# Attention values transposed on VectorE in 32 by 32 blocks, loaded block-wise, in a two-layer image kernel

## The chip, the cores and the metric

The kernel runs on one core of a Trainium2 chip. The core has TensorE (PE in the profile; its weight loads are PEld), VectorE (DVE), ScalarE (ACT), GpSimd (POOL) and SyncE (SP). SP does no arithmetic here: it issues most of the DMA transfers, one after another, in program order. The metric is the device time of one launch in microseconds (us); less is better. All data is float32.

## The reference

Two layers over an image x of 48 channels and 256 by 256 pixels, each added to its own normalised input. The change lies in the attention of layer 0. What it computes, cut to what matters:

```python
# _gn: each of 16 groups of 3 channels loses its mean and is divided by its deviation
qkv = einsum('bchw,oc->bohw', _gn(x), w_qkv)      # 144 channels
qkv = dwconv3x3(qkv, w_dw)
q, k, v = split(qkv, 3, axis=1)
# unfold: image (4 pixels of padding around) cut into 4 by 4 patches;
# head h gets 6 channels x 16 pixels = 96 rows, one column per patch
q, k, v = heads(q), heads(k), heads(v)            # 8 heads of [96, patches]
q, k = l2norm(q), l2norm(k)                       # over the 96 rows
attn = softmax(einsum('bhcn,bhcm->bhnm', q, k) * temperature, axis=-1)
out = einsum('bhcn,bhnm->bhcm', v, attn)          # [96, patches] of each head
x = x + einsum('bchw,oc->bohw', fold(out), w_proj)
# layer 1: three products over width, height and channels in 64 by 64 windows
x = x + sum_t einsum('bcphqw,wW,hH,cC->bCpHqW', windows(_gn(x)), Ws[t], Hs[t], Cs[t])
```

There are 64 by 64 = 4096 patches that hold pixels (`NT`). The patches of the padding hold zeros and enter each softmax sum as a constant (`NBORDER` times exp of minus the maximum).

## The kernel before

The kernel has three stages. The first normalises x, makes the 144 channels and, for head 0, the depthwise convolution, and writes the patches to DRAM tensors `qkv[h]`. The second is the attention, head by head, with the convolution of the next head woven in. The third is the projection and layer 1.

`qkv[h]` has the shape [3, 3, 7, 96, 640]: which of q, k, v is the second index; each 96-row matrix is cut by patches into 7 chunks (`CH`) of 576 columns (`CN`; the last has 640, and the last 64 columns are left unused in the others). A row of patches, 64 columns of all seven chunks, is written by one `Depthwise(h, r)` object; r runs over 0 to 9, where r = 9 fills only the last 64 columns of the last chunk.

The attention runs over `for h in range(8)`, `for g in range(16)`. One pass g (about 22 us) takes two blocks of 128 query patches. All keys of a head (8 tiles `kt`, of 512 patches each) stay in SBUF, 14 buffers in all, so that six of the next head's fit beside them. The parts of a pass, with the names used below:

- `scores` (L563): 24 matmuls (L337) of 128 queries with 4096 keys into four `big` tiles of PSUM (3 buffers), each followed by an exponential on ACT (L572) into `e`. A pass has two of these: first `scores(h, 2g+1)`, then already the first block of the next pass, `scores(h, 2g+2)`. The queries of pass g lie in `qt`, two buffers, loaded two passes ahead (L674).
- `normalised` (L581): VectorE sums the exponentials and scales the block's 128 by 96 values by the reciprocal: `vn`. It reads `vT`, the values with patches on partitions.
- `load_value` and `turn` (L546, L552): the values lie in `qkv[h]` with the 96 rows outside and patches inside. `load_value` brings 512 patches as a [96, 512] tile `vt` (2 buffers, one or two transfers according to where a chunk ends). `turn` makes four 96 by 128 transposes on TensorE into a PSUM tile `pst` and copies it with ACT to `vT` [128, 4, 96] (9 buffers).
- `weigh` (L594): for each k of 4, 32 matmuls (L601) of the two blocks' exponentials with `vn` into a `big` tile, then VectorE adds it to the sum `oacc` in SBUF (L612; L610 in the first pass of a head). With three `big` buffers, the fourth tile of a pass can be started only when VectorE has added the first.

Between these stand the convolution of head h+1 (`Depthwise`: load of three `pad` pieces at L205, first tap on ACT, eight taps on VectorE at L228, sum of squares, norm, scaling, then the stores to `qkv[h+1]` by POOL at L295) and, in head 0 only, the `Strip` objects (L162) that make the 108 channels of heads 2 to 7: each loads `xs` (L171), runs matmuls into a `big` tile (L177) and stores `ot` to DRAM (L189).

The order on every engine is the one in which the code stands, since the loop lies inside `tc.manual_schedule()` (only what comes ahead of it, `load_query(0, 0)`, the keys and first values of head 0, may be moved by the scheduler). A transfer waits on SP until its buffer is free and its data is written; everything behind it on SP waits too. On SP a pass issues in this order: values of this pass, keys of the next head, queries of pass g+2 (they wait until `scores(h, 2g+1)` has finished with the buffer), `pad`, and in head 0 the strips' stores and loads.

In head 0, `load_value(0, m)` and `turn(0, m)` stand ahead of the loop for m = 0 and 1, and in passes 1 to 6 for m = 2 to 7. For the other heads they stand in passes 11 to 14 of the head before (`CR + 2 <= g < CR + 6`), two tiles in each pass; keys of the next head are loaded in passes 12 to 14 (two tiles each) and in pass 15. `turn` stands behind both `scores` and both `normalised` of its pass, ahead of the four `weigh`.

The transfers that SP issues take their completion semaphores in turn from a set of eight, so that a transfer also waits for the one eight places before it.

Of the kernel before, what the change touches and what calls it, by code (L numbers as in the profile page):

```python
# [8 lines left out]
F32 = mybir.dt.float32  # L9
# [14 lines left out]
HD = C * KK // NH  # L24
# [4 lines left out]
CH = 7  # L29
CR = 9  # L30
# [15 lines left out]
def conv_preact_kernel(  # L46
# [15 lines left out]
    nc = tc.nc  # L62
# [11 lines left out]
    CN = CR * PX  # L74
    t1 = [dram.tile([(h1 - h0) * HC, TR, W + 2], F32, name=f"t1_{h0}") for h0, h1 in GROUPS]
    qkv = [dram.tile([3, 3, CH, HD, CN + PX], F32, name=f"qkv{h}") for h in range(NH)]
# [5 lines left out]
    ident = const.tile([128, 128], F32, name="ident")  # L82
# [15 lines left out]
    for s in range(2):  # L98
        r = slice(s * C, (s + 1) * C)
        for h in range(NH if s == 0 else H0):  # L100
            o = s * M0 + h * HC if h < H0 else (h - H0) * HC
            nc.gpsimd.dma_start(
                out=(wq[r] if h < H0 else wr[0:C])[:, o : o + HC].rearrange("c (z e) -> c z e", z=3),
                in_=w_qkvT.rearrange("c (z h e) -> h c z e", z=3, h=NH)[h],
# [4 lines left out]
    for z in range(3):  # L109
        for j in range(CH):  # L110
            p = (z * CH + j) * 6
# [50 lines left out]
    class Strip:  # L162
# [5 lines left out]
        def load(self):  # L168
            self.xs = cv.tile([64 + C, 2, W], F32, name="xs", bufs=3)
            for s, rows in enumerate(both_halves(xc, 2 * self.j, 2)):  # L170
                nc.sync.dma_start(out=self.xs[s * 64 : s * 64 + C], in_=rows)  # L171
# [129 lines left out]
    NB = NT // 128  # L301
# [101 lines left out]
    with tc.tile_pool(name="xn", bufs=1) as xnp, tc.tile_pool(name="cst", bufs=1) as cst, tc.tile_pool(  # L403
        name="nps", bufs=2, space=PSUM
# [123 lines left out]
    with tc.tile_pool(name="ahead", bufs=2) as ah, tc.tile_pool(name="ae", bufs=3) as ae, tc.tile_pool(  # L528
# [2 lines left out]
        MB = 8  # L531
        NK = NB // MB
        NLATE = 1
        RP = TP // PX * KS
        NG = NB // G
        keys, queries, values, oaccs = {}, {}, {}, {}
# [8 lines left out]

        def load_value(h, m):  # L546

            vt = ah.tile([HD, 4 * 128], F32, name="vt")
            load(vt, qkv[h][2, 2], m * 512, (m + 1) * 512)
            values[h, m] = vt  # L550

        def turn(h, m):  # L552
            ps = one.tile([128, 4, HD], F32, name="pst", tag="one")
            for i in range(4):
                nc.tensor.transpose(ps[:, i, :], values[h, m][:, i * 128 : (i + 1) * 128], ident[:HD, :HD])  # L555
            vT = ah.tile([128, 4, HD], F32, name="vT", bufs=9)
            nc.scalar.copy(vT, ps)
            values[h, m] = vT

        e0 = ao.tile([128, NH * NB], F32, name="e0")  # L560
# [20 lines left out]
        def normalised(h, nb, e, zs):  # L581

            b = h * NB + nb
            zt = asm.tile([128, 1], F32, name="zt")
            nc.vector.tensor_reduce(zt, zs, AX.X, ALU.add)  # L585
            zu = asm.tile([128, 1], F32, name="zu")
            nc.vector.scalar_tensor_tensor(zu, e0[:, b : b + 1], float(NBORDER), zt, ALU.mult, ALU.add)
            rz = asm.tile([128, 1], F32, name="rz")
            nc.vector.reciprocal(rz, zu)
            vn = asm.tile([128, HD], F32, name="vn")  # L590
            nc.vector.tensor_scalar_mul(vn, values[h, nb // 4][:, nb % 4, :], rz)
            return e, vn

        def weigh(h, g, blocks, k):  # L594
# [32 lines left out]
        load_query(0, 0)  # L627
        for m in range(NM):
            load_key(0, m, (nc.scalar, nc.sync, nc.gpsimd)[m % 3])
        for m in range(2):  # L630
            load_value(0, m)
            turn(0, m)

# [6 lines left out]
        with tc.manual_schedule():  # L642
            load_query(0, 1)
            block = scores(0, 0)
            for h in range(NH):
                more = h + 1 < NH
                rows = {r: Depthwise(h + 1, r) for r in range(CR + 1)} if more else {}
                for g in range(NG):
                    p, d, n = rows.get(g - 2), rows.get(g - 1), rows.get(g)

                    if not more and g == 0:
# [1 line left out]
                        early = ExitStack()  # L653
                        pe = early.enter_context(tc.tile_pool(name="pe", bufs=1, side="right"))
                        xts = [pe.tile([P2, RP, W], F32, name=f"xt{t}") for t in range(NX)]
                    if h == 0 and 0 < g <= 6:
                        load_value(0, g + 1)
                    if more and CR + 2 <= g < CR + 6:
                        for m in range(2):
                            load_value(h + 1, (g - CR - 2) * 2 + m)  # L660
                    if more and CR + 3 <= g < CR + 6:
                        for m in range(2):
                            load_key(h + 1, (g - CR - 3) * 2 + m)
# [28 lines left out]
                    if g == 0 and rows:  # L692
                        rows[0].load()

                    if h == 0 and 0 < g <= 6:
                        turn(0, g + 1)
                    if more and CR + 2 <= g < CR + 6:
                        for m in range(2):
                            turn(h + 1, (g - CR - 2) * 2 + m)
                    if g == 0 and h > 0:  # L700
                        for m in range(6, 8):
                            store(h - 1, m)
# [293 lines left out]
```

## Time and profile before

| | us |
|---|---|
| median of 3 runs (3668.67 to 3677.88) | 3673.2 |
| span of the profiled execution | 3669.5 |
| PE busy, of the span | 3466.2 |
| PEld busy | 2907.3 |
| VectorE busy | 2139.8 |
| ScalarE busy | 1873.5 |
| POOL busy | 542.7 |
| mean granted TensorE clock | 0.976 of full |

The span runs from the first to the last instruction of the profiled execution; no further time is listed for that execution. In the table of 40 slices the PE row shows 9 tenths or more from slice 4 to slice 34 (about 290 to 3210 us): this is the attention. The first three slices and the last five belong to the other stages. Busy shares overlap, since engines work side by side. An engine that is not busy may still set the time of what waits for it.

### The profile page before, as it was taken

The numbers are of one execution on the slowest core, as the hardware profiler recorded it, in microseconds if no ns is written. First come the engines' busy times: TensorE is split into PE (matmuls) and PEld (weight loads), VectorE is DVE, ScalarE is ACT, GpSimd is POOL, SyncE is SP. The second block draws the span as 40 slices with busy tenths as digits, with TensorE's granted clock in tenths as the row PEclk, the third lists the DMA queues.
The fourth block names the chain that finished last, engine by engine and source line by source line (L and its number), as shares of the span: only waits on it lengthen the run. The fifth ranks groups of instructions, "written<-read, shape, count | busy, mean of one in ns | idle before, by whom it ended". The sixth has DMA issues, their size and how long they took to land.

```text
span 3669.5 us, 100344 instructions
## 1 busy us (share of the span) xinstructions
PE 3466.2 (94%) x44252; PEld 2907.3 (79%) x44252; DVE 2139.8 (58%) x3518; ACT 1873.5 (51%) x2747; POOL 542.7 (15%) x630
## 2 busy tenths in 40 slices
PE   2869999999999999999999999999999999965998
PEld 1337788889988888889899988888899888833776
DVE  5464674179628952895389439934993222267654
ACT  0235676566646654665466556655664444400332
POOL 2030211012211211121112112211221100010011
PEclk9989999999999999999999999999999999976999
DMA  7455665533322332333233323332333220089674
GB/s 161 154 131 147 180 171 168 158 97 92 94 72 82 98 90 80 83 93 87 78 82 92 94 76 87 86 93 71 94 84 87 65 53 19 15 213 240 116 136 93
DMA packets 275427, 386.49 MB, mean 105 GB/s; under 512 B 77330, under 2 KB 211842, under 8 KB 270952
## 3 DMA queue, kind: packets, MB, share of 16 engines
q1 hardware_dynamic: 235942, 264.95, 27.3%
q0 software_dynamic: 35552, 106.40, 12.6%
q10 hardware_dynamic: 3490, 8.64, 1.1%
q8 instruction: 350, 5.73, 0.7%
q14 instruction: 93, 0.76, 0.1%
HBM read 234.76 MB, written 144.90 MB: 103 GB/s over the span
## 4 chain that ended last, share of the span: by engine, by line
PE 84%; DVE 3%; issue 2%; DMA 2%; ACT 1%; SPq 0%; POOL 0%; ACTq 0%; POOLq 0%; DVEq 0%
PE big L337 37%; PE big L601 36%; PE pb L896 4%; PE pa L874 2%; PE pc L913 2%; DVE acc L228 1%; PE big L177 1%; PE pt L618 1%; PE pn L247 1%; DMA pot<-os__70 1%; PE pst L555 1%; DMA x1s<-pxt 0%; DMA kt<-qkv 0%; DMA t<-ot 0%; DVE ss L243 0%
## 5 line engine op out<-in xcount | busy, mean ns | idle before, releaser
L572 ACT ACTIVATE e<-big,nmx 128x1024 f32<-128x1024 f32 x1024 | 1143.9, 1117 | 878.4 <-PE big L337 617.5
L337 PE MATMUL big<-kt,qt 128*128 128x512 f32 x6144 | 1437.5, 393 | 30.2 <-DMA kt<-qkv 29.3
L601 PEld LDWEIGHTS big<-vn,e 128*64 128x64 f32 x32768 | 1358.6, 137 | 57.8 <-ACT e L572 30.6
L601 PE MATMUL big<-vn,e 128*64 128x96 f32 x32768 | 1388.9, 247 | 6.5 <-DVE oacc L612 3.0
L337 PEld LDWEIGHTS big<-kt,qt 128*128 128x128 f32 x6144 | 1146.3, 188 | 277.3 <-issue 29.2
L612 DVE TENSOR_TENSOR oacc<-big,oacc 128x768 f32<-128x768 f32 x480 | 453.5, 954 | 713.4 <-PE big L601 713.4
L228 DVE SCALAR_TENSOR_TENSOR acc<-pad,dwt,acc 126x1024 f32<-126x1024 f32 x592 | 765.6, 1293 | 39.5 <-ACT acc L209 23.7
L295 POOL DMA_DIRECT2D qkv<-o x72 | 52.7, 732 | 1242.2 <-ACT o L279 1242.2
L585 DVE TENSOR_REDUCE zt<-zs 128x1 f32<-128x4 f32 x256 | 38.5, 150 | 335.7 <-ACT e L572 335.7
L289 POOL TENSOR_TENSOR ol<-o,oh 126x1024 fp32r<-126x1024 f32 x78 | 184.6, 2367 | 311.6 <-DVE ss L243 238.9
L572 ACT ACTIVATION_READ_ACCUMULATOR e<-big,nmx 128x1 f32 x1024 | 196.4, 192 | 0.0
L903 ACT COPY lyt<-pb 128x512 f32<-128x512 f32 x144 | 84.3, 586 | 201.6 <-PE pb L896 201.6
L881 DVE TENSOR_TENSOR lzt<-pa,cbias 128x864 f32<-128x864 f32 (+1 forms) x88 | 137.0, 1628 | 85.3 <-PE pa L874 85.3
L279 ACT COPY o<-acc 126x1024 f32<-126x1024 f32 x74 | 158.6, 2143 | 0.0
L896 PEld LDWEIGHTS pb<-wsb,lzt 128*64 128x64 f32 x2304 | 125.9, 138 | 29.4 <-issue 19.7
L896 PE MATMUL pb<-wsb,lzt 128*64 128x128 f32 x2304 | 141.9, 279 | 2.8 <-issue 1.6
L623 POOL DMA_DIRECT2D os__70<-oo x128 | 64.9, 513 | 534.4 <-ACT oo L621 533.8
L790 PE MATMUL pps<-pot,wp 96*96 96x512 f32 x128 | 78.0, 777 | 55.2 <-DMA pot<-os__70 44.3
L239 ACT ACTIVATE sq<-acc 126x1024 f32<-126x1024 f32 x74 | 78.2, 1057 | 101.6 <-DVE acc L228 101.6
L180 ACT ACTIVATE ot<-big,bias 108x1024 f32<-108x1024 f32 x64 | 68.2, 1110 | 111.1 <-PE big L177 62.8
L209 ACT ACTIVATE acc<-pad,dwt 126x1024 f32<-126x1024 f32 x74 | 84.1, 1137 | 79.9 <-DMA pad<-t 79.9
L243 DVE TENSOR_REDUCE ss<-sq 126x64 f32<-126x1024 f32 x80 | 97.5, 1219 | 24.6 <-ACT sq L239 24.6
(127 smaller groups left out, 1904.8 us busy)
## 6 DMA issues: line engine op xcount, KB each, us to landing
pad<-t SPq DMA_DIRECT2D x238, 254.0 KB
t<-ot SPq DMA_DIRECT2D x128, 217.7 KB
qkv<-ol POOLq DMA_DIRECT2D x78, 336.0 KB, 6.4
qkv<-oh POOLq DMA_DIRECT2D x70, 336.0 KB, 5.6
qt<-qkv SPq DMA_DIRECT2D x176, 96.0 KB
xs<-in_x_dram SPq DMA_DIRECT2D x128, 96.0 KB
os__70<-oo POOLq DMA_DIRECT2D x128, 96.0 KB, 2.1
pot<-os__70 SPq DMA_DIRECT2D x16, 768.0 KB
```

The source lines that it names most:

```text
L209: nc.scalar.mul(self.acc, self.pad[:, 0:KS, 0:W], dwt[:, self.h, 0:1])
L228: nc.vector.scalar_tensor_tensor(self.acc, self.pad[:, dy : dy + KS, dx : dx + W], dwt[:, self.h, tap : tap + 1], self.acc, ALU.mult, ALU.add,
L243: nc.vector.tensor_reduce(self.ss, self.sq.rearrange("p a (x b) -> p x a b", b=KS), AX.XY, ALU.add)
L279: nc.scalar.copy(self.o.rearrange("p (a b) x -> p a b x", a=KS), self.acc.rearrange("p a (x b) -> p a b x", b=KS))
L289: eng.tensor_sub(self.ol, self.o, self.oh.bitcast(F32))
L337: nc.tensor.matmul(ps[:, i, :], lhsT=qt[:, r, q0 : q0 + 128], rhs=kts[2 * j + i][:, r // 2, :], start=(r == 0), stop=(r == 2),)
L572: nc.scalar.activation(e[:, j * 1024 : (j + 1) * 1024], ps.rearrange("p a b -> p (a b)"), AF.Exp, bias=nmx[:, b : b + 1], accum_out=zs[:, ...
L601: nc.tensor.matmul(ps[p : p + 64, j // 4, j % 4 * HD : (j % 4 + 1) * HD], lhsT=e[:, mb * 128 + p : mb * 128 + p + 64], rhs=vn, start=(i == 0),
L612: nc.vector.tensor_add(oaccs[h, k], ps[:, :, : 4 * HD], oaccs[h, k])
L881: nc.vector.tensor_tensor(zv[:, :, y0 : y0 + n, :], pa[:, :, : n * T3 * C].rearrange("p s (y k) -> p s y k", y=n), cbias.rearrange("p (u v ...
L896: nc.tensor.matmul(pb[s * WS : (s + 1) * WS, i, :], lhsT=zts[u][:, t * C + c + i, :], rhs=wsb[:, t, :], start=True, stop=True,)
L903: nc.scalar.copy(yt[:, t, :], pb.rearrange("p i x -> p (i x)"))
```

## The change

Values are loaded eight blocks of 128 patches at a time (`VB = 8`, 1024 patches), so that a head needs four loads instead of eight. The new tile `vt` is [128, 8, 3, 32] in one buffer: partition 32p + c holds, for block i and row group b, row 32b + c of the 32 patches that will stand on partitions 32p to 32p + 31 of that block. One transfer carries 32 rows by up to 8 blocks by 32 patches, and it is cut where a chunk of `qkv` ends. `turn` is then one VectorE instruction on [128, 768], which transposes each 32 by 32 square where it stands: it gives `vT` [128, 8, 96] (5 buffers). The four TensorE transposes and the ACT copy of each old `turn` are gone, and with them the PSUM tile `pst`.

The loads of head 0 now stand ahead of the loop for m = 0 and in passes 1 to 3 for m = 1 to 3; those of the next head in passes 11 to 14, one in each. `turn` keeps its place in the pass. The numbers of transfers by load are 24, 36, 36 and 24, so 120 in a head where there were 14.

```diff
+        VB = 8
...
         def load_value(h, m):
 
-            vt = ah.tile([HD, 4 * 128], F32, name="vt")
-            load(vt, qkv[h][2, 2], m * 512, (m + 1) * 512)
+            vt = ah.tile([128, VB, 3, 32], F32, name="vt", bufs=1)
+            for p in range(4):
+                at = [m * VB * 128 + i * 128 + p * 32 for i in range(VB)]
+                chunk = [min(n // CN, CH - 1) for n in at]
+                for j in sorted(set(chunk)):
+                    i0, i1 = chunk.index(j), VB - chunk[::-1].index(j)
+                    n0 = at[i0] - j * CN
+                    for b in range(3):
+                        src = qkv[h][2, 2, j, b * 32 : (b + 1) * 32, n0 : n0 + 32]
+                        src = bass.AP(src.tensor, src.offset, [src.ap[0], [128, i1 - i0], [1, 32]])
+                        nc.sync.dma_start(out=vt[p * 32 : (p + 1) * 32, i0:i1, b, :], in_=src)
             values[h, m] = vt
 
         def turn(h, m):
-            ps = one.tile([128, 4, HD], F32, name="pst", tag="one")
-            for i in range(4):
-                nc.tensor.transpose(ps[:, i, :], values[h, m][:, i * 128 : (i + 1) * 128], ident[:HD, :HD])
-            vT = ah.tile([128, 4, HD], F32, name="vT", bufs=9)
-            nc.scalar.copy(vT, ps)
+
+            vT = ah.tile([128, VB, HD], F32, name="vT", bufs=NB // VB + 1)
+            nc.vector.transpose(vT.rearrange("p i c -> p (i c)"), values[h, m].rearrange("p i b n -> p (i b n)"))
             values[h, m] = vT
...
-            nc.vector.tensor_scalar_mul(vn, values[h, nb // 4][:, nb % 4, :], rz)
+            nc.vector.tensor_scalar_mul(vn, values[h, nb // VB][:, nb % VB, :], rz)
...
-        for m in range(2):
-            load_value(0, m)
-            turn(0, m)
+        load_value(0, 0)
+        turn(0, 0)
...
-                    if h == 0 and 0 < g <= 6:
-                        load_value(0, g + 1)
-                    if more and CR + 2 <= g < CR + 6:
-                        for m in range(2):
-                            load_value(h + 1, (g - CR - 2) * 2 + m)
+                    if h == 0 and 0 < g < NB // VB:
+                        load_value(0, g)
+                    if more and CR + 2 <= g < CR + 2 + NB // VB:
+                        load_value(h + 1, g - CR - 2)
...
-                    if h == 0 and 0 < g <= 6:
-                        turn(0, g + 1)
-                    if more and CR + 2 <= g < CR + 6:
-                        for m in range(2):
-                            turn(h + 1, (g - CR - 2) * 2 + m)
+                    if h == 0 and 0 < g < NB // VB:
+                        turn(0, g)
+                    if more and CR + 2 <= g < CR + 2 + NB // VB:
+                        turn(h + 1, g - CR - 2)
```

## The prediction

> **What bounds the kernel now.** I read the chain of waits first, then two stretches of it, then SP's own timeline for the same stretch, then the rows of the transfers.
>
> ```profile
> PE 84%; DVE 3%; issue 2%; DMA 2%; ACT 1%; SPq 0%; POOL 0%; ACTq 0%; POOLq 0%; DVEq 0%
> ```
>
> TensorE carries the chain in the attention, with almost no idle time: whatever is taken from PE there is gained, whatever makes PE wait is lost. The merged chain of head 1 shows a pass with two turns and, beside it, one without:
>
> ```profile
> 991.03 11.11 PE big L337 x48
> 1002.15 0.66 PE pst L555 x8
> 1002.81 10.71 PE big L601 x256
> 1013.52 11.11 PE big L337 x48
> ...
> 1128.36 10.96 PE big L337 x48
> ...
> 1150.39 10.96 PE big L337 x48
> ```
>
> The pass with turns lasts 1013.52 - 991.03 = 22.49 us, the one without 22.03. PE never waits for `vt` here: the timeline of SP tells why.
>
> ```profile
> 956.67 8.96 SPq L311 DMA_DIRECT2D vt<-qkv  x3
> 974.25 6.01 SPq L311 DMA_DIRECT2D qt<-qkv  x12
> 980.35 1.93 SPq L311 DMA_DIRECT2D vt<-qkv  x4
> 982.39 11.35 SPq L311 DMA_DIRECT2D kt<-qkv  x12
> 996.74 4.01 SPq L311 DMA_DIRECT2D qt<-qkv  x6
> 1002.51 1.71 SPq L311 DMA_DIRECT2D vt<-qkv  x4
> 1004.27 10.57 SPq L311 DMA_DIRECT2D kt<-qkv  x16
> ```
>
> Values take SP 1.7 to 1.9 us a pass, keys 10 to 11, queries 3 to 6. SP is free 5 to 6 us of 22, and only because the values are cheap. (The 8.96 us of the first row are a wait: its second transfer needs the convolution's store that POOL issues at 961.2, and goes at 964.8.)
>
> **What the change removes.** 256 transposes on PE. In passes 11 to 14 of seven heads: 28 x 0.46 = 12.9 us. In head 0, eight turns of 0.3 to 0.6 us each (0.49 us busy in the timeline): about 2.6. Together -15.5 us. The 64 ACT copies (470 ns each) gave nothing to wait for: ACT is 51% busy and its exponentials wait for PE.
>
> **What it adds on VectorE.** 32 transposes of [128, 768]. No row has one; the nearest is L612's add on the same size (954 ns), the dearest POOL's subtraction of 1024 elements (2367 ns). I take 0.95 us, 30 us in all; in passes 11 to 14 VectorE is busy 5.2 us of 22.5, so this by itself hides; at 2.4 us it would add 1.4 to each of the two late turns of a head below, 20 in all at most, which the range holds. The wait it brings is what matters: the turn waits for all 24 or 36 transfers, and behind it on VectorE stands the add L612 that frees the `big` buffer of the fourth `weigh`.
>
> **What it adds on SP.** 960 transfers for 112, at 128 bytes a run. The engines don't mind: the packet records put a 256-byte packet at 18 ns, and 3072 packets over 16 engines are then at most 3.5 us a load. SP's issue decides. Its rows:
>
> ```profile
> L311 SPq DMA_DIRECT2D vt<-qkv x112: 303/418/730, 288.0 to 2815.9; - x112
> L824 ACTq DMA_DIRECT2D csn<-in_Cs_dram x2: 343/402/462, 3209.4 to 3209.8; - x2
> L857 SPq DMA_DIRECT2D lrt<-x1s x16: 574/866/6269, 3371.1 to 3616.8; - x16
> ```
>
> (min/median/max in ns.) The new form has three dimensions on both sides. From below: 0.30 us (a plain transfer that finds the queue empty). Plain ones in a run go at 0.42 and start 0.47 apart. From above: `lrt`, three dimensions of 64 rows, 0.87 + 0.05 between two. Nearest is `csn`, 48 rows by 3 by 48: the second, with one in front of it, took 0.462, so 0.50 apart. I take **0.50 us a transfer**: 12 us for a load of 24, 18 us for one of 36. Completion records of the old `vt` come 2.3 us after issue in the median; I take 2.2 after the last issue has ended.
>
> The Trainium skill speaks against the change: "DMA: Bandwidth & Descriptors", Rules for kernel authors, says that transfers under 64 KB pay mostly overhead, and its fit is 2.0 us a transfer. By it, unoverlapped, 848 more transfers would be some 1700 us, an estimate from that page. The 16 keys in 10.57 us above show that such overhead overlaps, so only the issue enters my sum.
>
> **A head, step by step**, in us from the start of pass 11 (968.7), a pass being 22.0 without turns: 5.5 for each `scores`, then four `weigh` of 2.64. VectorE reaches the turn at 7.8 of a pass; PE wants the first add by 18.9. Keys go at 0.65 (10.57/16), queries at 0.51.
> - Load 0: from -3.8 (964.8, the store) to 8.2; landed 10.4; turned 11.3. No loss. Queries to 14.3.
> - Load 1: to 32.3, landed 34.5, turned 35.5; PE wants the add by 40.9. No loss. 12 keys to 40.1, queries to 43.2.
> - Load 2: to 61.2, landed 63.4, turned 64.3, added 65.3; wanted at 62.9: PE waits 2.4. 16 keys to 71.6, queries to 74.6, landed 76.8; the second `scores` of pass 14 wants them at 73.9: 3.0 (rounded).
> - Load 3: to 86.6, landed 88.8, added 90.8, wanted 90.3: 0.5. 16 keys to 97.0, the next head's first queries landed at 102.3, wanted at 99.3: 3.0. Key tile 6: 0.4.
>
> SP had 5 to 6 us free a pass and is given 10 to 17 more: the backlog surfaces as late turns and late queries. About 9.5 us a head, seven heads: +66.
>
> **Head 0** has no slack, since the strips hold SP:
>
> ```profile
> 324.04 2.00 SPq L311 DMA_DIRECT2D vt<-qkv  x2
> 329.49 6.56 DVE L228 SCALAR_TENSOR_TENSOR acc<-pad,dwt,acc 126x1024 f32<-126x1024 f32 x5
> 336.06 0.96 DVE L612 TENSOR_TENSOR oacc<-big,oacc 128x768 f32<-128x768 f32 x1
> 338.58 1.97 PE L177 MATMUL big<-xs,wr 48*108 48x512 f32 x8
> ```
>
> In pass 1 the load starts at 324.0, ends at 342.0, is landed at 344.2 and turned at 345.2, and L612 ends at 346.1. The second strip's run wanted that buffer at 339.5: 6.6 late, and some 2 more for L243 and the second add behind it. Twice 8.6 (passes 1, 2), and 2.6 for the 24 of pass 3: +20. At the start, 24 transfers at 288 for three (12 for 1.5 us) put the queries of `load_query(0, 1)` 10.5 us back; they had landed 3.7 ahead of their `scores`: at 296.6 (issued by 294.4, completion records 2.0 to 2.2 later) against 300.3 (41 matmuls in 9.57 us from 295.69, the first 20 of them another block's): +7.
>
> **The clock.** In the projection a PE gap of 4.17 us is followed by half clock:
>
> ```profile
> 3257.80:3262.00 4.20, 0.05 (x1) 0.00 (x0) 4.20 (x6) 0.00 (x0) 0.00 (x0) 0.94 1.10 176
> 3262.00:3268.30 6.30, 6.28 (x8) 2.27 (x9) 6.27 (x4) 0.00 (x0) 0.00 (x0) 0.50 0.90 235
> ```
>
> (bounds, length, PE, PEld, DVE, ACT, POOL busy, granted clock, DMA share, GB/s.) So a stall of over 4 us costs 3 us more: three of them in head 0, +9. Those of 3 us in the other heads: nothing taken; at most 14 x 3 = 42, which the range holds. "TensorE: Matmul & The Clock Gate", What's actually happening, puts the drop at about 3.4 us of idleness and the return after about 3.4 us of work; by that rule the three would cost some 5 instead of 9, an estimate from that page, and the shorter ones nothing.
>
> **Sum**: -15.5 + 7 + 20 + 66 + 9 = +86.5 on a span of 3669.5, so 3756. The median of the runs lies 3.7 above the span, so **3760**.
>
> **Rivals.**
> - *The issue is cheap: the turn leaves PE and nothing waits* (the other side). Needs 0.30 us a transfer all through: then load 1 of pass 1 is added at 338.9, ahead of 339.5, about 3 us of stalls stay in head 0 and 2 at the start, and no backlog forms in the others. -15.5 + 5 gives 3663, with none of these stalls 3658. For it: 303 ns exists. Against: only in transfers that find SP idle. Above 0.30 it is gone. Chance 0.10.
> - *Only head 0 pays.* At 0.47 a transfer and 0.56 a key (0.42 and 0.595 alternating, plus gaps) the same ladder leaves 1.6 us a head: -15.5 + 6 + 17 + 11 + 9 gives 3701; at 0.42 about 3680. For it: 0.47 is the plain form's spacing, and part of the keys' 0.65 is waiting behind POOL's stores. Chance 0.22.
> - *The third dimension is dear*, as in `lrt`: at 0.92 the ladder gives 60 a head (422), 60 in head 0, 17 at the start and some 60 of half clock: 4217; at 0.67 30 a head: 3940. For it: 0.87 follows 0.58 regularly. Against: eight times the runs of a new transfer. Chance 0.18.
> - That the change doesn't do what it says is excluded: the built program has no `pst` and 32 transposes on VectorE.
>
> **How the numbers follow.** The forecast (0.47 to 0.58 us a transfer, 3700 to 3860) has 0.50. Changes within 0.3% (11 us) can't be told from none. Faster than 3662 needs the first rival nearly whole: 0.09. 3662 to 3684: the low end of the second and rest of the first, 0.09. Slower 0.82. The range, 3676 to 3930, leaves out 0.1 below and 0.1 above.
>
> **What would show it.** After: a `vt` spacing on SP near 0.5 in runs of 24 and 36; no `pst`; VectorE idle ahead of L565's transpose, released by DMA `vt`, longest in passes 1 and 2; PE waiting for L612's add (now L620) and for DMA `qt` in passes 13 to 15, none in 1 to 10 of heads 1 and later, which should last 22.0 as before. Head 7 loads no values for a next head and should not change. I am wrong if SP's spacing is 0.3 or 0.9, if a stall moves the strips' loads too, or if the DMA engines, not the issue, delay the landing.

## The result, and the profile after

The changed kernel takes **3920.9 us** (median of 4 runs, 3913.2 to 3926.7) against 3674.1 of the kernel before: a ratio of **1.067** (95% interval 1.065 to 1.069), 6.7% slower. Slower was forecast, and the range held the time, but the forecast of 3760 had +86 where +247 was measured. The profiled execution has a span of 3917.7 us, 248.2 more than before.

The chain that ended last (the page's part 4), first by engine, then by line:

```profile
PE 61%; SPq 16%; DMA 5%; issue 5%; DVE 5%; ACT 1%; POOL 0%; ACTq 0%; DVEq 0%; POOLq 0%
PE big L609 26%; PE big L337 25%; SPq L559 11%; SPq L311 4%; PE pb L901 4%; DVE acc L228 2%; PE pa L879 2%; PE pc L918 2%; PE big L177 1%; DMA t<-ot 1%; DMA qt<-qkv 1%; PE pt L626 1%; DMA x1s<-pxt 1%; DMA pad<-t 1%; DVE oacc L620 1%
```

PE had 84% of this chain; now SP's issuing has 16%, and 11 of them are L559, the new value transfers. Where PE stands idle (busy us, mean ns of one, idle us ahead of it and its main releaser; the same groups of the page, and the new turn):

```profile
L609 PE MATMUL big<-vn,e 128*64 128x96 f32 x32768 | 1425.8, 250 | 115.2 <-DVE oacc L620 113.3
L337 PE MATMUL big<-kt,qt 128*128 128x512 f32 x6144 | 1466.9, 398 | 54.8 <-DMA qt<-qkv 44.4
L565 DVE STREAM_TRANSPOSE vT<-vt 128x768 f32<-128x768 f32 x32 | 31.3, 979 | 375.8 <-DMA vt<-qkv 333.1
L177 PE MATMUL big<-xs,wr 48*108 48x512 f32 x256 | 78.7, 692 | 51.3 <-DMA xs<-in_x_dram 44.4
```

The idle time ahead of these three PE groups was 6.5, 30.2 and 1.4 us before: +183 now. They also run longer for the same count of matmuls: 1388.9, 1437.5 and 64.8 us before, +80 now. These 263 us, less some 19 for the transposes that left PE, make 244 of the 248. The turn itself is cheap, 0.979 us; but VectorE stands 376 us ahead of it. How this looks in head 1, SP first (start, length, transfers, count):

```profile
1073.37 15.50 SPq L559 DMA_DIRECT2D vt<-qkv  x24
1088.97 7.27 SPq L311 DMA_DIRECT2D qt<-qkv  x12
1096.34 22.63 SPq L559 DMA_DIRECT2D vt<-qkv  x36
1119.09 7.22 SPq L311 DMA_DIRECT2D kt<-qkv  x12
1126.40 3.10 SPq L311 DMA_DIRECT2D qt<-qkv  x6
1129.61 20.27 SPq L559 DMA_DIRECT2D vt<-qkv  x36
```

From 1073 to 1199 SP has no gap over 0.35 us left. The four loads of the head take 15.50, 22.63, 20.27 and 15.84 us for 24, 36, 36 and 24 transfers: 0.62 us each (0.61 over all 32 loads). VectorE in the same stretch (the bracket is the idle time before the row and who ended it):

```profile
1120.52 0.98 DVE L565 STREAM_TRANSPOSE vT<-vt 128x768 f32<-128x768 f32 x1 [14.03 <-DMA vt<-qkv]
1121.42 2.65 DVE L620 TENSOR_TENSOR oacc<-big,oacc 128x768 f32<-128x768 f32 x3
```

And PE:

```profile
1109.73 8.14 PE L609 MATMUL big<-vn,e 128*64 128x96 f32 x192
1122.40 5.39 PE L609 MATMUL big<-vn,e 128*64 128x96 f32 x64 [4.52 <-DVE oacc L620]
1127.72 11.46 PE L337 MATMUL big<-kt,qt 128*128 128x512 f32 x48
```

The load ends at 1118.97 on SP, the turn starts at 1120.52, three adds that had queued up behind it run at once, and PE, out of `big` buffers since 1117.9, goes on. Its next 64 matmuls take 5.39 us, twice the usual. The windows say why (bounds, length, PE, PEld, DVE, ACT, POOL busy, granted clock, DMA share, GB/s):

```profile
1117.90:1122.40 4.50, 0.00 (x0) 0.00 (x1) 1.88 (x3) 0.00 (x0) 0.00 (x0) 0.90 0.46 126
1122.40:1125.00 2.60, 2.60 (x32) 2.60 (x34) 1.67 (x2) 0.00 (x0) 0.00 (x0) 0.50 0.45 118
1127.00:1128.00 1.00, 1.00 (x11) 0.78 (x10) 0.16 (x1) 0.00 (x0) 0.00 (x0) 0.50 0.67 181
1129.00:1130.00 1.00, 1.00 (x6) 0.80 (x5) 0.48 (x3) 0.31 (x1) 0.00 (x0) 1.00 0.45 139
```

The clock stays at 0.50 for some 6 us after the stall. So a late turn makes PE wait and then run at half speed for a while.

Where the 248 us lie, by the starts of the score matmuls of each pass (worked out from the traces, after minus before, us; the 1.4 us that are missing in the sum lie behind the attention):

```
                   loop    head 0        head 0         heads 1-6   head 7
                   start   passes 0-10   passes 11-15   together
measured            +3.2      +52.6         +52.6         +140.0     -1.6
of it, by pass:  head 0: 0 +8.0, 1 +9.6, 2 +23.2, 3 +7.0, 4 +2.9, 5 +2.0
                 head 0: 11 +8.2, 12 +13.7, 13 +16.5, 14 +12.0, 15 +2.2
                 head 1: 1 to 10 0.0, 11 -0.7, 12 +6.6, 13 +8.1, 14 +3.3, 15 +5.1
```

### The profile page after: what moved, and what is told of

It reads as the page before. It is cut to its first block, busy times and chain, and to the rows that moved or that the text cites. A ratio compares the mean times of both kernels' runs of the same rounds, so it can differ in the third digit from the quotient of the medians.

```text
span 3917.7 us, 100771 instructions
## 1 busy us (share of the span) xinstructions
PE 3525.0 (90%) x43996; PEld 2938.1 (75%) x43996; DVE 2163.6 (55%) x3550; ACT 1850.2 (47%) x2683; POOL 542.7 (14%) x630
## 3 DMA queue, kind: packets, MB, share of 16 engines
q1 hardware_dynamic: 337062, 265.01, 27.0%
q0 software_dynamic: 35552, 106.40, 11.9%
## 4 chain that ended last, share of the span: by engine, by line
PE 61%; SPq 16%; DMA 5%; issue 5%; DVE 5%; ACT 1%; POOL 0%; ACTq 0%; DVEq 0%; POOLq 0%
PE big L609 26%; PE big L337 25%; SPq L559 11%; SPq L311 4%; PE pb L901 4%; DVE acc L228 2%; PE pa L879 2%; PE pc L918 2%; PE big L177 1%; DMA t<-ot 1%; DMA qt<-qkv 1%; PE pt L626 1%; DMA x1s<-pxt 1%; DMA pad<-t 1%; DVE oacc L620 1%
## 5 line engine op out<-in xcount | busy, mean ns | idle before, releaser
L609 PE MATMUL big<-vn,e 128*64 128x96 f32 x32768 | 1425.8, 250 | 115.2 <-DVE oacc L620 113.3
L609 PEld LDWEIGHTS big<-vn,e 128*64 128x64 f32 x32768 | 1391.8, 139 | 178.0 <-DVE oacc L620 128.4
L337 PE MATMUL big<-kt,qt 128*128 128x512 f32 x6144 | 1466.9, 398 | 54.8 <-DMA qt<-qkv 44.4
L337 PEld LDWEIGHTS big<-kt,qt 128*128 128x128 f32 x6144 | 1164.2, 191 | 318.5 <-issue 51.1
L620 DVE TENSOR_TENSOR oacc<-big,oacc 128x768 f32<-128x768 f32 x480 | 448.5, 950 | 488.0 <-PE big L609 488.0
L565 DVE STREAM_TRANSPOSE vT<-vt 128x768 f32<-128x768 f32 x32 | 31.3, 979 | 375.8 <-DMA vt<-qkv 333.1
L180 ACT ACTIVATE ot<-big,bias 108x1024 f32<-108x1024 f32 x64 | 69.3, 1111 | 202.3 <-DMA t<-ot 102.9
L177 PE MATMUL big<-xs,wr 48*108 48x512 f32 x256 | 78.7, 692 | 51.3 <-DMA xs<-in_x_dram 44.4
```

The lines of the kernel that those rows point to most:

```text
L177: nc.tensor.matmul(ps[:M1, s, :], lhsT=wr[r], rhs=self.xs[r].rearrange("p a b -> p (a b)"), start=True, stop=True)
L337: nc.tensor.matmul(ps[:, i, :], lhsT=qt[:, r, q0 : q0 + 128], rhs=kts[2 * j + i][:, r // 2, :], start=(r == 0), stop=(r == 2),)
L609: nc.tensor.matmul(ps[p : p + 64, j // 4, j % 4 * HD : (j % 4 + 1) * HD], lhsT=e[:, mb * 128 + p : mb * 128 + p + 64], rhs=vn, start=(i == 0),
L620: nc.vector.tensor_add(oaccs[h, k], ps[:, :, : 4 * HD], oaccs[h, k])
```

## The experiments

Theory 1 is that SP's issue of 960 transfers is what is paid. Its rivals: the turn's place on VectorE (2), the bytes or packets on the DMA engines (3). In the diffs `-` is the changed kernel, if nothing else is said. The differences given for each run are against the kernel before, by the columns above; two numbers for head 0 are its passes 0 to 10 and 11 to 15.

**Few large transfers, same turn.** All 32 turns stay; the tile is filled by 4 to 6 transfers.

```diff
-            for p in range(4):
...
-                        nc.sync.dma_start(out=vt[p * 32 : (p + 1) * 32, i0:i1, b, :], in_=src)
+            to = vt.rearrange("p i b n -> p (i b n)")
+            n0 = min(m * VB * 128, NT - 768)
+            load(to[0:HD], qkv[h][2, 2], n0, n0 + 768)
+            load(to[HD:128], qkv[h][2, 2][:, 0:32], n0, n0 + 768)
```

> The turn on VectorE stays as in the changed kernel (32 of 128x768, waiting for a whole load), but a load's 393 KB come in 4 to 6 large plain transfers on SP instead of 24 or 36 small ones; the values stand in another arrangement, so the output is not the reference's. Theory 1 (SP's issue of 960 transfers makes the loss): SP is as free as before the change, so no PE wait for the adds behind the turn in passes 11 to 15 and next to none in head 0; 3655 to 3668 us, that is before less the 15.5 us of transposes and plus a few us in head 0. Theory 2 (the turn's place in VectorE's queue, or its one vt buffer, makes the loss, whatever fills the tile): the time stays at 3890 to 3920. Theory 3 (the bytes on the DMA engines): the bytes are the same, so 3850 to 3920.

Measured: 3652.0 us (one run; before 3672.6), 3 below what was expected; span 3649.9. Start -0.6, head 0 -2.0 and -1.7, heads 1 to 6 -15.9 together. Its groups of PE:

```profile
L337 PE MATMUL big<-kt,qt 128*128 128x512 f32 x6144 | 1437.0, 393 | 31.2 <-DMA kt<-qkv 29.2
L603 PE MATMUL big<-vn,e 128*64 128x96 f32 x32768 | 1387.6, 247 | 8.3 <-DVE oacc L614 4.8 <-DVE vn L593 1.9 <-ACT ot L180 1.6
```

Idle and busy times are within 2 us of those of the kernel before. With the same turns at the same places, and the same bytes, nothing is lost and 19.6 us of span are gained: theory 2 falls, and theory 3 as far as it speaks of bytes. A pass with turns went from 22.49 to 21.8 us.

**As many transfers, turned on TensorE.** Against the kernel before:

```diff
-            load(vt, qkv[h][2, 2], m * 512, (m + 1) * 512)
+            for p in range(4):
+                for b in range(3):
+                    n0 = m * 512 + p * 128
+                    load(vt[b * 32 : (b + 1) * 32, p * 128 : (p + 1) * 128],
+                         qkv[h][2, 2][:, b * 32 : (b + 1) * 32], n0, n0 + 128)
```

> The kernel before, transposes on TensorE kept, with nothing changed but that each of its value loads is cut into 12 or more plain pieces of 32 rows by up to 128 columns: as many transfers on SP as the changed kernel has. Theory 1 (SP's count): the loss comes without any work on VectorE: at 0.5 to 0.6 us a piece 3780 to 3920 us, with PE waiting for DMA vt and DMA qt. Theory 2 (the turn on VectorE): 3670 to 3690, within 0.5% of before.

Measured: 3779.5 us (one run), +107, at the lower end of what was expected; the cut makes 840 transfers. Head 0 +40.0 and +41.8, heads 1 to 6 +26.5. VectorE turns nothing here, so a loss needs no turn on it. Most of it lies in head 0, where the strips' transfers also go through SP. In heads 1 to 6 it is far smaller than the +140.0 of the changed kernel: 120 fewer transfers, their plain form, two buffers for `vt` and the turn's place on PE differ together, and no run separates them.

**As many transfers, but plain.** The source is one run of columns instead of blocks 128 apart:

```diff
-                        src = qkv[h][2, 2, j, b * 32 : (b + 1) * 32, n0 : n0 + 32]
-                        src = bass.AP(src.tensor, src.offset, [src.ap[0], [128, i1 - i0], [1, 32]])
...
+                        src = qkv[h][2, 2, j, b * 32 : (b + 1) * 32, n0 : n0 + (i1 - i0) * 32]
...
```

> The same 960 transfers of the same size on SP, but each source a plain 2-D block (32 rows by one run of 32 to 160 floats), no third dimension; the values stand in another arrangement, so the output is not the reference's. If the count and SP's fixed time per transfer make the loss (theory 1a), a transfer goes at 0.5 to 0.6 us all the same and the time is 3780 to 3900. If the 128-byte runs or the third dimension make the transfer dear (theory 1b), it goes at 0.43 to 0.47 and the time is 3680 to 3740. If the landing of 128-byte packets on the DMA engines is what is waited for (theory 3), SP's spacing stays at 0.62 and yet the time falls to about 3700.

Measured: 3827.3 us (one run). A load of 24 or 36 takes 0.54 or 0.56 us a transfer where the changed kernel's take 0.64 and 0.59. Head 0 +45.2 and +43.4, heads 1 to 6 +64.3. So as many plain transfers at the same places make about 155 of the 247 us; the third dimension, with its 128-byte runs, makes the other third through some 0.05 us a transfer. The issue row of the changed kernel (min/median/max ns):

```profile
L559 SPq DMA_DIRECT2D vt<-qkv x960: 302/430/2988, 291.0 to 3085.1; - x192
```

and of `plain_vt`:

```profile
L560 SPq DMA_DIRECT2D vt<-qkv x960: 302/419/2372, 288.9 to 2991.6; - x192
```

The medians hardly differ, and both are below the forecast's 0.50. The means don't follow them: in the changed kernel 71 of the 960 records are longer than 0.9 us, 1.42 in the mean; they add 0.07 to the mean of 0.548, to which the gap between two records adds 0.04. In `plain_vt` it is 74, and they add as much. Such long records weren't new: in the kernel before, 52 of the 384 key records on SP are longer than 0.9 us (median 0.458, mean 0.622), though none of the 112 value records is. The changed kernel's own excess sits in the 240 transfers of five blocks, 0.60 in the median, where those of one to four blocks have 0.42 to 0.43.

**The same transfers on POOL's queue.**

```diff
-                        nc.sync.dma_start(out=vt[p * 32 : (p + 1) * 32, i0:i1, b, :], in_=src)
+                        nc.gpsimd.dma_start(out=vt[p * 32 : (p + 1) * 32, i0:i1, b, :], in_=src)
```

> The changed kernel with its 960 value transfers issued by POOL's queue instead of SP's; nothing else moves. POOL's plain transfers in the trace take 0.51 us (the output rows of a head) to 1.05 us (the strided stores of queries and keys), and POOL is idle in passes 11 to 15. Theory 1 (SP's queue): SP is freed, the strips' loads, keys and queries run as before. At 0.5 us on POOL a load of 36 takes 18 us, it lands in its own pass, and the time is 3658 to 3690; at 1.05 a load of 36 takes 38 us, longer than a pass, and the loss comes back at 3850 or above through late turns alone, with no late queries. Theory 2 or 3 (the turn's place, or 128-byte packets on the DMA engines): 3900 at either price.

Measured: 3722.0 us, ratio 1.013 (1.010 to 1.016). Head 0 +3.3 and +8.7, heads 1 to 6 +36.3. Four fifths of the loss are gone with SP freed. What is left is neither of the two cases expected:

```profile
L559 POOL DMA_DIRECT2D vt<-qkv x960 | 525.7, 562 | 137.4 <-DVE vT L565 76.6
```

At 0.56 us a record, a load of 36 takes 21.1 us in the mean, as on SP (21.2). It fits in a pass, but the turn that waits for it stands 8 us into the pass. The Trainium skill, "DMA: Bandwidth & Descriptors", Issuing engine by pattern, calls the Sync and Scalar path generally the faster one. For a single transfer the rows agree (median 430 ns against 551); for a load of 36 they show no difference (0.59 us a transfer on both).

**Spread over the passes, then the same with a later turn.** The first moves three of a head's four loads and turns out of the crowded passes 11 to 14 and leaves one in pass 12; the second leaves its loads alone and moves only the turns, by one pass.

```diff
+                    if g in (1, 5, 9):
+                        load_value(h, g // 4 + 1)
+                    if more and g == CR + 3:
+                        load_value(h + 1, 0)
...
+                    if g in (1, 5, 9):
+                        turn(h, g // 4 + 1)
+                    if more and g == CR + 3:
+                        turn(h + 1, 0)
```

> The changed kernel's 960 transfers, all on SP and in the same form, moved in time: in every head value tiles 1, 2 and 3 are loaded and turned in passes 1, 5 and 9 of their own head (four passes ahead of their use), tile 0 in pass 12 of the head before. Theory 1 (SP's backlog in passes 11 to 15): heads 1 to 6 lose their 25 us of stalls each, since passes 1 to 10 have over 10 us of SP free; with 36 transfers at 0.62 in one pass the turn may still be 2 to 6 us late there. Head 0 keeps stalls of some 8 us at the start and in passes 1, 5, 9 and 12: 3665 to 3720. Theory 2 (the turn's place on VectorE): the same 32 waits elsewhere, 3850 or above.

The second, against the first:

```diff
-                    if g in (1, 5, 9):
+                    if g in (2, 6, 10):
                         turn(h, g // 4 + 1)
-                    if more and g == CR + 3:
+                    if more and g == CR + 4:
                         turn(h + 1, 0)
```

> The spread version with each turn one pass behind its load (loads in passes 1, 5, 9 and 12, turns in 2, 6, 10 and 13): the same 960 transfers, the same bursts of 24 and 36 on SP at the same places; only the deadline is later. If a burst of 36 at 0.6 us (22 us, landed 2 later) against a turn 8 us into the same pass made the 12 to 17 us that heads 1 to 6 of the spread version still lose, they now gain 2.7 each as with few transfers, and head 0 loses only what its bursts take from the strips' loads on SP (some 20 to 50): 3665 to 3710. If the bursts delay something else on SP (queries, keys, the convolution's rows), heads 1 to 6 stay slow and the time is over 3750.

Measured: `spread_vt` 3817.6 us (one run), well above what was expected: head 0 +53.4 and +11.4, heads 1 to 6 +75.7. `spread_late` 3744.7 (one run), also above what was expected, by 35: head 0 +54.0 and +11.7, heads 1 to 6 +9.3. Pass 1 of head 1 shows the difference. First SP's timeline of `spread_vt`,

```profile
812.45 24.21 SPq L559 DMA_DIRECT2D vt<-qkv  x36
```

then PE:

```profile
814.19 11.19 PE L337 MATMUL big<-kt,qt 128*128 128x512 f32 x48
825.31 8.14 PE L609 MATMUL big<-vn,e 128*64 128x96 f32 x192
839.82 5.39 PE L609 MATMUL big<-vn,e 128*64 128x96 f32 x64 [6.36 <-DVE oacc L620]
```

The same of `spread_late`, SP:

```profile
812.25 23.83 SPq L559 DMA_DIRECT2D vt<-qkv  x34
```

(the window shows 34 of its 36) and PE:

```profile
812.25 11.19 PE L337 MATMUL big<-kt,qt 128*128 128x512 f32 x48
823.38 10.78 PE L609 MATMUL big<-vn,e 128*64 128x96 f32 x256
```

The same burst, found by an idle SP at the start of the pass, stops PE for 6.36 us where a turn in the same pass waits for it, and not at all where the turn comes a pass later. So no backlog is needed: 36 transfers are longer than the time up to the add. Most of the burst's cost in heads 1 to 6 is its **deadline**. Head 0 is different: its loss didn't move with the turns. There the burst holds up the strips, as SP's timeline of `spread_late` shows in pass 5 of head 0:

```profile
451.14 27.59 SPq L559 DMA_DIRECT2D vt<-qkv  x36
481.93 1.98 SPq L189 DMA_DIRECT2D t<-ot  x4
483.96 2.45 SPq L171 DMA_DIRECT2D xs<-in_x_dram  x4
```

For 30 us no strip is stored or loaded, and pass 5 lasts 19.0 us longer than before.

**Head 0 as before.** `mixed_vt` takes the spread version and lets head 0 load in large transfers and turn on TensorE:

```diff
+            if h == 0:
+                to = vt.rearrange("p i b n -> p (i b n)")[:HD, :512]
+                load(to, qkv[h][2, 2], m * 512, (m + 1) * 512)
...
+            if h == 0:
+                ps = one.tile([128, 4, HD], F32, name="pst", tag="one")
+                for i in range(4):
+                    nc.tensor.transpose(ps[:, i, :], values[h, "vt"][:, i * 128 : (i + 1) * 128], ident[:HD, :HD])
...
```

> Head 0 loads and turns as before the change (large loads, transposes on TensorE); heads 1 to 7 load in small transfers and turn on VectorE, with the tiles in passes 12 (for the next head) and 1, 5 and 9. Theory 1: the strips' passes get back what they had, except pass 12 of head 0, which has 24 small transfers (some 8 us), and the seven heads keep the gain of the transposes less late turns at the 36 transfers: 3658 to 3690. Theory 2: no better than 3800.

Measured: 3775.7 us, ratio 1.027 (1.024 to 1.030): not as expected, since heads 1 to 6 keep the late turns of `spread_vt` (+80.2). Head 0 is as forecast by theory 1: +4.9 in passes 0 to 10 where `spread_vt` had +53.4, and +11.8 in 11 to 15, all of it in pass 12 with its 24 transfers for head 1.

**Fewer transfers by another order of the queries.** A block takes every second patch of its 256, so that one transfer brings 32 rows of all three row groups by 64 patches.

```diff
-                    lhsT=qt[:, r, q0 : q0 + 128],
+                    lhsT=qt[:, r, q0 // 128 : 256 : 2],
...
+                    src = qkv[h][2, 2, j].rearrange("(b c) n -> c b n", b=3)[:, :, n - j * CN : n - j * CN + 64]
+                    dst = to[p * 32 : (p + 1) * 32, u * 192 : (u + 1) * 192].rearrange("p (b n) -> p b n", b=3)
+                    nc.sync.dma_start(out=dst, in_=src)
```

> Loads and turns in the same passes as in the changed kernel and on SP, but 16 transfers for a load instead of 24 or 36 (512 in all): a block of 128 queries takes every second patch of its 256, so that a partition quarter's run is 64 patches and one transfer takes all three row groups. Theory 1: at 0.55 to 0.6 us a load takes 9 to 10 us; the ladder of the prediction, with 16 in place of 24, 36, 36, 24, gives stalls of 0 to 5 us a head, and head 0 some 10 to 40 in all: 3665 to 3725. Theory 3 (what counts is the number of DMA packets, or the turn): over 3800; the packets are halved with runs of 256 bytes, so at least half of the loss, 3790.

`perm4_vt` does the same pass by pass: `load_value(h, g + 2)` behind `load_query(h, g + 2)`, and `turn(h, g + 1)` in every pass.

> The same arrangement, and each pass loads and turns only its own 256 patches, two passes ahead, behind the queries in SP's order: 4 transfers and a turn of 128x192 a pass, 512 and 128 in all. Theory 1: SP is given 2.4 us in each pass, in passes 11 to 14 about what the old values took (1.7 to 1.9), so no backlog forms anywhere, no turn waits, and the transposes' time is gained whole: 3652 to 3668, faster than before by 0.2 to 0.5%. Theory 2 (a turn on VectorE in front of the adds costs by itself): 128 turns, slower than before. If the weight loads of every second column are slow on TensorE, the scores take longer than 5.5 us and the time is far above 3700.

Measured: `perm_vt` 3726.4 us (one run), just above what was expected; `perm4_vt` 3706.1, ratio 1.008 (1.005 to 1.012), not faster as expected but slower. In `perm_vt` PE doesn't wait over 0.8 us anywhere in heads 1 to 6, and a load of 16 takes 8 to 15 us (10.8 in the mean); head 0 still pays +17.7 and +19.3. Both pay in every pass for something else, the weight loads of every second column. The groups of L337 in `perm4_vt`:

```profile
L337 PE MATMUL big<-kt,qt 128*128 128x512 f32 x6144 | 1477.2, 398 | 32.9 <-DMA qt<-qkv 21.9
L337 PEld LDWEIGHTS big<-kt,qt 128*128 128x128 f32 x6144 | 1182.4, 194 | 284.6 <-issue 31.2
```

194 ns a load instead of 188, and 0.3 us in each of the 128 passes (22.03 to 22.33), 38 us in all. 3706 less these 38 is 3668, about the kernel before; a version without them wasn't run.

**More transfers than the changed kernel, evenly.** Blocks are consecutive again; every pass loads its own 256 patches in 8 transfers, two passes ahead.

```diff
-            vt = ah.tile([128, VB, 3, 32], F32, name="vt", bufs=1)
+            vt = ah.tile([128, 2, 3, 32], F32, name="vt", bufs=3)
             for p in range(4):
...
+                for i in range(2):
+                    n = g * 256 + i * 128 + p * 32
+                    j = min(n // CN, CH - 1)
+                    src = qkv[h][2, 2, j].rearrange("(b c) n -> c b n", b=3)[:, :, n - j * CN : n - j * CN + 32]
+                    nc.sync.dma_start(out=vt[p * 32 : (p + 1) * 32, i], in_=src)
...
                         load_query(h, g + 2)
+                        load_value(h, g + 2)
```

> More transfers than the changed kernel has, 1024, all on SP, blocks of 128 queries as they were, but 8 in every pass, two passes ahead of use, behind the queries, and a turn of 128x192 in every pass. If the count of transfers as such made the loss (the sum over all of 0.6 us is 610 us of SP), it comes back: 3850 to 3950. If it is a burst against its deadline, 4.9 us of SP in each pass fit in what SP has free (5 to 6 us in passes 12 to 14, over 10 in passes 1 to 10): heads 1 to 6 gain 2.7 each, head 0 loses 20 to 40 with the strips: 3665 to 3700.

`pool8` issues these 8 transfers from POOL instead of SP (`nc.sync` becomes `nc.gpsimd`).

> As the run before it, the 8 transfers of a pass on POOL's queue instead of SP's. POOL is given 4.5 us a pass at the 0.56 that the earlier run on POOL showed; it is busy 5 us of 22 in passes 1 to 10 and idle in 11 to 15, so no turn is late, and SP is freer than before the change: 3648 to 3662, faster than before by 0.3 to 0.7%, near the 3652 of the version with few large transfers. If POOL's waits (for the convolution's rows, and for the last key tile in pass 15) hold the values behind them, single passes stall by 5 to 20 us: 3680 to 3800.

Measured: `even8` 3702.5 us (one run), 2.5 above what was expected: heads 1 to 6 -10.2, head 0 +33.4 and +7.7. With 1024 transfers against 960, all on SP, at 0.56 us each, the loss of those heads is gone: it isn't the count as such. Nor is it the packets (theory 3): SP's queue moves 338,086 here against 337,062 in the changed kernel. What stays is head 0. `pool8` **3657.2 us**, ratio 0.994 (0.992 to 0.996): faster than the kernel before, as expected, with heads 1 to 6 at -15.7, as with few large transfers. Its value row:

```profile
L555 POOL DMA_DIRECT2D vt<-qkv x1024: 545/552/693, 267.6 to 3117.3; - x171
```

A transfer is dearer here than the median one on SP, and in heads 1 to 6 it costs nothing: POOL has the time, and the turn comes a pass later. Head 0 loses 9.1 in passes 0 to 10 (5.7 each in passes 6 and 10, 3.2 gained in pass 4); in those two passes PE waits 3.2 and 4.1 us for the copy of a strip on ACT (L180), and why that copy is late stays open.

## Why the prediction was right in its sign and wrong in its size

**The transposes on PE** ("28 x 0.46 = 12.9 us", with head 0 -15.5). The step was right, the size low: PE's passes 11 and later shortened by 0.67 each, 28 x 0.67 = 18.8. I had compared them with the 22.03 of passes that hold a convolution row's matmul L247, which passes 11 to 14, taken from score to score, don't have; the right figure, 21.81 us, stood in head 7.

**VectorE's turn** (0.95 us): measured 0.979. Head 7 and passes 1 to 10 of heads 1 to 6: as forecast; the DMA engines didn't delay the landing either (1.4 us after an issue's end in the median, where 2.2 were taken).

**"I take 0.50 us a transfer"** is the step that failed first. The changed kernel's loads took 0.62 in head 1. The median was forecast well (0.43, with 0.04 between two); the mean was not, for one record in 14 is 1.4 us long, which a row of min/median/max doesn't show and two records of `csn` can't, and the quarter of the transfers with five blocks takes 0.60. The ladder charged the keys by the mean of a long run (0.65), in which such long records stand, and the values by `csn`. By the ladder, the 36 of load 1 at 0.50 landed at 34.5 for an add at 40.9, "No loss". At 0.62, behind 12 queries, they left SP at 1118.97, the turn began at 1120.52, and PE stood for 4.52 us in pass 12. `plain_vt` shows how steep this is: at 0.55 a head loses 13 us (64.3 + 15.9 over six), at 0.62 it loses 26 (140.0 + 15.9 over six). The ladder's total stood: worked again with 0.62 it gives 23.6 us a head (an estimate), and head 1 lost 25.1 (22.4, and the 2.7 that its transposes gave). Its single waits didn't: it makes the 23.6 of waiting alone, and head 1 waited 16.6.

**"Seven heads: +66"** failed twice over. The 9.5 a head are 26 in heads 1 to 6. And head 0's passes 11 to 15 were counted like the others', though the strips hold SP there too: +52.6, where 9.5 less the transposes was forecast. The prediction had said that head 0 "has no slack", and drawn it only for passes 1 to 3. In each of passes 11 to 14 PE waits 5.8 to 10.2 us for a strip's input `xs`, 32.3 in all, which is the prediction's own sign of being wrong ("if a stall moves the strips' loads too"). `mixed_vt` and `even8` show SP's strips as the cause: pass 12 alone, with 24 transfers, costs 12 us there, and next to nothing in heads 1 to 6 of `spread_late`.

Of the some 160 us by which the forecast was too low, 94 lie in heads 1 to 6 (46 forecast with the transposes, 140 measured) and 67 in head 0 with its start (41 forecast, 108 measured).

**The clock** ("three of them in head 0, +9. Those of 3 us in the other heads: nothing taken") is a second term that was off: the three PE groups run 80 us longer. In place of three stalls over 4 us the attention has 21 in the trace, eight in head 0 and 13 in heads 1 to 6; before it had one, of 4.07 at its start. Of head 1's 25.1 us, 16.6 are stalls (4.52, 5.73, 3.44 and 2.89), and 8.5 mostly the slower matmuls after them. But the ladder with 0.62, which has no clock term, comes out at nearly the whole 25.1. SP issues almost without a gap there, so slower matmuls can fill time in which PE would otherwise have waited for SP; how much of the 80 us is a cost of its own no run separates.

Where the clock changes can be read in windows of 3.41 us (columns as above):

```profile
1118.11:1121.52 3.41, 0.00 (x0) 0.00 (x0) 1.00 (x2) 0.00 (x0) 0.00 (x0) 1.00 0.40 101
1121.52:1124.93 3.41, 2.53 (x32) 2.53 (x34) 2.55 (x3) 0.00 (x0) 0.00 (x0) 0.50 0.55 155
1124.93:1128.34 3.41, 3.41 (x38) 3.10 (x36) 0.50 (x1) 0.00 (x0) 0.00 (x0) 0.50 0.40 110
1128.34:1131.75 3.41, 3.41 (x16) 2.81 (x15) 1.11 (x5) 1.90 (x3) 0.00 (x0) 1.00 0.31 85
...
1176.13:1179.54 3.41, 1.77 (x44) 1.58 (x40) 0.08 (x1) 0.00 (x0) 0.00 (x0) 1.00 0.26 52
1179.54:1182.96 3.42, 1.63 (x40) 1.63 (x42) 3.42 (x4) 0.00 (x0) 0.00 (x0) 1.00 0.44 112
...
1189.78:1193.20 3.42, 0.53 (x2) 0.19 (x1) 0.75 (x4) 1.21 (x2) 0.00 (x0) 1.00 0.81 219
1193.20:1196.61 3.41, 3.32 (x9) 2.65 (x9) 0.00 (x0) 0.73 (x1) 0.00 (x0) 0.50 0.40 100
1196.61:1200.02 3.41, 3.41 (x17) 2.73 (x15) 0.00 (x0) 2.66 (x5) 0.00 (x0) 1.00 0.44 122
```

All changes of the clock in this trace lie on one grid of 3.41 us. Here a window with no matmul time, or 0.53 us of it, is followed by 0.50; those with 1.77 and 1.63, between which the stall of 3.44 is divided, are not. So the stall of 2.89, nearly all in one window, brought 3.4 us at 0.50, and the longer one of 3.44 none. After the 4.52 the return took 5.9 us: the rest of the window in which the stall ended, and one full window. The Trainium skill, "TensorE: Matmul & The Clock Gate", What's actually happening, lets the clock fall after an idle window of about 3.4 us and return after a busy one, and calls the window free-running. The trace agrees, with "idle" including the window with 0.53. The prediction had taken the 3.4 us for the length of the stall; its 3 us for a stall over 4 us stands (half of the 5.9), the number of stalls was wrong.

**The mechanism** was named rightly, the late turns and the late queries, and PE's waits in the heads are the ones listed (L620's add, DMA `qt`). Only VectorE's longest waits ahead of the turn aren't in passes 1 and 2 of head 0 (9.8 and 11.6 us) but in the later heads (up to 17.2). But "the backlog surfaces" put the weight on SP's total. `spread_vt` and `spread_late` show that a burst loses against its deadline without any backlog, and `even8` that a larger total loses nothing in heads 1 to 6. In the changed kernel itself backlog and deadline act together; how the 26 us of a head divide between them wasn't separated.

**The rivals.** Cheap issue, and a loss in head 0 alone, are excluded by 0.62 and by heads 1 to 6. The dear third dimension had 0.67 and 3940, nearest to the result in size; `plain_vt` leaves it about a third of the loss; the rest comes with plain transfers too. The 2.0 us a transfer that the prediction sets beside its sum is given by the Trainium skill, "DMA: Bandwidth & Descriptors", Anatomy of one DMA, for the GpSimd path and not for SP; on either path a load of 36 took 0.59 us a transfer, so leaving it out of the sum was right.

## What to carry to other kernels

Price a group of DMA issues by the mean of long runs, rare long records included, and set it against the time from the load's place in the program to the first consumer: a group that is longer than this stalls even with its queue idle ahead. Before a transform moves to another engine, ask what layout it demands and whose queue brings that layout; cut the loads into even shares, a pass or two ahead of use, on a queue that has the time. A stall can also have an aftermath: here 183 us of waits came with 80 us of slower matmuls, part of which may only have taken the place of waiting.

## What the runs showed of the hardware

- One value transfer in 14 takes SP 0.9 to 3 us to issue, 1.4 in the mean, in long groups and in short ones (76 of 1024 in `even8`); none of the 112 value records before was over 0.9, but 52 of its 384 key records were. What causes them stays open.
- None of POOL's records is that long: 545/552/693 ns in `pool8`.
- In the changed kernel's trace the granted clock changes only on a grid of 3.41 us: a stall of 2.89 us that lay in one window was followed by half clock, one of 3.44 across two was not.
- SP's queue counts 3072 packets for a load of 128-byte runs and 16 for each transfer, 113,664 in all (337,062 less the 223,398 that stay in `pool_vt`; 960 x 16 + 32 x 3072); POOL's queue counts 30,720 for the same 960 transfers (66,272 less 35,552), 32 each.
- A weight load of every second float32 column takes 194 ns instead of 188.
- Turning 128x768 took 979 ns on VectorE, and 128x192, with the same blocks, 373: four small ones cost half as much again.
